# The second LSTM step of window pairs as seven half-size products in place of eight, with four groups' rows parked in DRAM

## The chip, the cores and the metric

The kernel runs on one core of one Trainium2 chip. The metric is the device time of one execution in microseconds; the median of three runs of the kernel before is 2540.0 us (2535.27 to 2540.68). The profile shown is of one execution with a span of 2539.1 us at a mean granted TensorE clock of 0.993, so the clock plays no part here.

## What is computed

The input is a batch of 128 graphs of 64 nodes with 256 features, 8192 rows in all, in fp32. Four layers follow one another, each with a residual sum and a layer norm: two kinds of graph convolution, a convolution with LSTMs over windows of nodes, and an attention. The change lies in the third layer, whose core is

```python
for p in range(1, 4 + 1):
    nw = Tv // p
    wins = h[:, :nw * p, :].reshape(Bv * nw, p, Hd)
    last = _lstm_last(Wih[p - 1], Whh[p - 1], bih[p - 1], bhh[p - 1], wins)
    h = h.at[:, arange(nw) * p + (p - 1), :].set(last)
# one step of _lstm_last
g = x_t @ Wih.T + h @ Whh.T + bias          # 1024 gate columns out of 256 + 256
i, f, gg, o = split(g, 4)
c = sigmoid(f) * c + sigmoid(i) * tanh(gg)
h = sigmoid(o) * tanh(c)
```

For p = 2 the 64 nodes of a graph make 32 windows of two nodes. The first step has no previous state, so it needs `Wih` alone. The second step needs `Wih` and `Whh`, and it is this step that changes.

## The kernel before

The rows are cut into 64 tiles of 128 and handled in 16 **groups** of four tiles, that is eight graphs or 512 rows. All rows lie in the SBUF tile `X` (L649) from start to end and are updated in place.

The program has two stages. In the first, `layer0` runs for all groups, two at a time, with a Strassen scheme of its own for its largest product. There a `norms` list holds small pieces of layer-norm work; one piece is popped for each of the 14 products of a group (L832). Beside it `eigen`, a long chain of small VectorE instructions, works out a 64 x 64 eigenbasis. In the second stage, from about 860 us on, `group(g)` takes each group through `layer1`, `layer2` and `layer3`; three groups are under way at once (`WAYS = 3`).

**What sets the order.** TensorE's order is written out by hand (L1205 to L1219): each group is a generator that yields the time at which its next piece may start, on a clock `now` that the program advances by its own price for each matmul (L717). The loop picks the first group that is ready, in the order in which the groups began, and if none is ready it moves the clock to the one that is ready soonest. The waiting times are constants, such as `CELL[256] = 3.8` us after the last matmul of an LSTM step with 256 moving columns. TensorE itself knows nothing of `now`: it runs its list in order and waits only where an operand or a buffer isn't ready. The orders of VectorE and ScalarE are left to the framework's scheduler in this stage.

**The LSTM** is `lstm(hT, p, first, nw)`, L991. `hT` holds the group's nodes transposed, with features on the partitions. For each step `t` it goes through eight `units` (L1005), one for each gate and half of the gate's 256 columns. A unit takes one PSUM bank from `ps4`, fills it with two matmuls of `wi` and, from the second step on, two of `wh` (L1026, L1029), each with all `n = 8 * nw` moving columns. Then one ScalarE tanh reads the bank with bias (L1030), and VectorE works out `c` and `h` from the gate tiles (L1034 to L1041, L1051). For p = 2 there are 256 moving columns. Every bank of the LSTM is first written in full and then read, and it has no second writer before it is given back. The pool `psb` has eight banks[...]; `pw` has five tiles with tag `w`.

## Time and profile before

| what | us | share of the span |
|---|---|---|
| TensorE matmul, busy | 2494.8 | 98% |
| TensorE weight load, busy | 2196.2 | 86% |
| VectorE, busy | 1407.8 | 55% |
| ScalarE, busy | 1090.6 | 43% |
| DMA, mean rate | 12 GB/s | |

In the stage that holds the change, between 900 and 2300 us, VectorE is busy for about 92 us in each 200 and ScalarE for about 90. The DMA queues are all but silent after the inputs and weights have been loaded, at the start and at 845 to 870 us.

A fp32 matmul call of the program appears as two MATMUL instructions in the profile: the second step of p = 2 has 8 units x 2 calls of `whh` for 16 groups, 256 calls, and the profile lists 512 such instructions. The duration of one matmul in the profile overlaps that of the next, so what one costs on the way is the distance from start to start. A group of instructions is listed as line, engine, operation, output and inputs with their shapes and a count; then the busy time, the mean duration of one in ns, and the idle time just before them with what ended it.

### The profile page before, as it was taken

Reading aid. Unit: us, or ns where it says so; the run is one execution under the profiler, and the core shown is the slowest. Engines: PE = TensorE matmul, PEld = TensorE weight load, DVE = VectorE, ACT = ScalarE, POOL = GpSimd, SP = SyncE. Lnnn points to the kernel's source line nnn. Section 1 sums busy time; section 2 is a strip of 40 time slices with the busy share of each in tenths; the row PEclk is TensorE's granted clock in tenths of the full one; section 3 lists DMA queues with packets and bytes.
Section 4 is the critical chain, followed back from the end, with each engine's and each line's share of the span. In section 5 each row is a group of like instructions: output and inputs, shape, how many; then the busy total and the mean of one; then the engine's idle time right before and its main releaser. Section 6 shows DMA issues by size and latency. Waiting matters only on the chain.

```text
span 2539.1 us, 39015 instructions
## 1 busy us (share of the span) xinstructions
PE 2494.8 (98%) x15020; PEld 2196.2 (86%) x15020; DVE 1407.8 (55%) x4996; ACT 1090.6 (43%) x2706; POOL 134.2 (5%) x316
## 2 busy tenths in 40 slices
PE   9999999999999999999999999999999999999997
PEld 7788887888878889998989889898998998978996
DVE  6888777778885433454453543544445345353235
ACT  2344333433333344445344444444444534535454
POOL 0000000000000100000000000000000000010001
PEclk9999999999999999999999999999999999999998
DMA  6000000000000300000000000000000000000000
GB/s 219 1 1 1 1 1 1 1 1 1 1 1 1 117 1 1 10 9 1 9 9 1 9 1 10 9 1 9 1 9 9 1 9 9 1 9 1 1 1 26
DMA packets 24634, 32.09 MB, mean 13 GB/s; under 512 B 2176, under 2 KB 21376, under 8 KB 24448
## 3 DMA queue, kind: packets, MB, share of 16 engines
q1 hardware_dynamic: 24096, 29.32, 3.4%
q8 instruction: 118, 1.93, 0.3%
q14 instruction: 68, 0.56, 0.1%
q10 hardware_dynamic: 352, 0.28, 0.0%
HBM read 21.20 MB, written 8.39 MB: 12 GB/s over the span
## 4 chain that ended last, share of the span: by engine, by line
PE 91%; DVE 5%; POOL 2%; issue 1%; DMA 0%; ACT 0%; SPq 0%; ACTq 0%; POOLq 0%; DVEq 0%
PE ps L716 88%; PE ps L926 2%; POOL ln_rs L554 1%; DVE X L564 1%; DVE ln_st L551 1%; DVE D L51 1%; PE ps L1146 1%; PE pc L93 1%; DMA X<-in_x_dram 0%; POOL ln_rs L553 0%; DVE tw L51 0%; DVE ln_mv L552 0%; DVE X L1176 0%; DVE X L986 0%; DVE X L1096 0%
## 5 line engine op out<-in xcount | busy, mean ns | idle before, releaser
L716 PE MATMUL ps<-w,wih 128*128 128x256 f32 (+2 forms) x4992 | 894.0, 319 | 1.8 <-DVE w L1051 1.8
L716 PEld LDWEIGHTS ps<-w,wih 128*128 128x128 f32 x4992 | 760.9, 191 | 47.8 <-issue 5.7
L1030 ACT ACTIVATE gates<-ps,cbi 128x128 f32<-128x128 f32 (+2 forms) x1248 | 499.3, 410 | 523.3 <-PE ps L716 516.2
L716 PE MATMUL ps<-hs,whh 128*128 128x128 f32 (+2 forms) x3072 | 540.5, 303 | 6.2 <-DVE hs L1041 6.2
L716 PEld LDWEIGHTS ps<-hs,whh 128*128 128x128 f32 x3072 | 453.9, 191 | 32.9 <-issue 11.2
L1036 DVE SCALAR_TENSOR_TENSOR gates<-gates 128x256 f32<-128x256 f32 (+2 forms) x256 | 89.3, 349 | 297.4 <-ACT gates L1030 297.4
L716 PE MATMUL ps<-aw,h 128*128 128x256 f32 x1024 | 227.2, 379 | 0.0
L716 PEld LDWEIGHTS ps<-aw,h 128*128 128x128 f32 x1024 | 192.9, 190 | 25.9 <-ACT h L725 0.5
L725 ACT ACTIVATE h<-h 128x512 f32<-128x512 f32 x128 | 80.5, 629 | 170.0 <-DVE h L51 169.8
L1039 ACT ACTIVATE gates<-c 128x128 f32<-128x128 f32 (+2 forms) x288 | 98.1, 341 | 114.1 <-DVE c L1038 87.9
L1034 DVE SCALAR_TENSOR_TENSOR c<-gates,c 128x128 f32<-128x128 f32 (+2 forms) x192 | 62.6, 326 | 139.4 <-ACT gates L1030 138.2
L1051 DVE SCALAR_TENSOR_TENSOR w<-gates 128x256 f32<-128x256 f32 (+2 forms) x160 | 59.6, 376 | 108.5 <-PE ps L716 73.5
L716 PE MATMUL ps<-ss,tw 128*128 128x256 f32 x512 | 117.9, 380 | 0.0
L716 PE MATMUL ps<-ss,aw 128*128 128x256 f32 x512 | 117.3, 379 | 0.0
L716 PE MATMUL ps<-m,aw 128*128 128x256 f32 x512 | 117.1, 380 | 0.0
L716 PE MATMUL ps<-aw,m 128*128 128x512 f32 x256 | 114.8, 594 | 0.0
L1041 DVE SCALAR_TENSOR_TENSOR hs<-gates 128x128 f32<-128x128 f32 (+2 forms) x192 | 62.6, 326 | 93.6 <-ACT gates L1039 52.4
L553 POOL TENSOR_SCALAR ln_rs<-ln_mv 128x2 f32<-128x2 f32 x96 | 26.2, 273 | 1558.4 <-DVE ln_mv L552 1557.9
L716 PEld LDWEIGHTS ps<-ss,aw 128*128 128x128 f32 x512 | 96.6, 190 | 12.8
L716 PEld LDWEIGHTS ps<-ss,tw 128*128 128x128 f32 x512 | 96.3, 190 | 12.9 <-issue 0.2
L564 DVE TENSOR_SCALAR X<-X,ln_mv,ln_rs 128x256 f32<-128x256 f32 x176 | 64.7, 410 | 75.9 <-POOL ln_rs L554 75.9
L716 PEld LDWEIGHTS ps<-m,aw 128*128 128x128 f32 x512 | 95.6, 190 | 12.6 <-issue 0.5
(294 smaller groups left out, 3107.4 us busy)
## 6 DMA issues: line engine op xcount, KB each, us to landing
X<-in_x_dram SPq DMA_DIRECT2D x30, 256.0 KB, 6.3
out_dram<-X SPq DMA_DIRECT2D x28, 256.0 KB, 2.1
wih<-in_c_ih_dram SPq DMA_DIRECT2D x4, 1024.0 KB, 7.2
aw<-in_a_w_dram SPq DMA_DIRECT2D x3, 1024.0 KB, 10.3
whh<-in_c_hh_dram SPq DMA_DIRECT2D x3, 1024.0 KB, 9.4
out_dram<-X SPq DMA_DIRECT2D x8, 128.0 KB, 1.7
aw<-in_a_w_dram SPq DMA_DIRECT2D x1, 512.0 KB, 5.8
cw<-in_c_w_dram SPq DMA_DIRECT2D x2, 256.0 KB, 5.1
```

Source lines behind the costliest of these rows:

```text
L51: return getattr(self.engine, name)(out, *args, **kw)
L553: nc.gpsimd.tensor_scalar(rs, mv[:, :, 1], EPS, None, op0=ALU.add)
L564: nc.vector.tensor_scalar(x[:, t, :], x[:, t, :], mv[:, t, 0:1], rs[:, t:t + 1], op0=ALU.subtract, op1=ALU.mult)
L716: PE.matmul(out, lhsT, rhs, start=start, stop=stop)
L725: S.activation(dst, src, AF.Relu)
L926: PE.transpose(out, in_, ident)
L1030: S.activation(gate[q][:, h, :], pp, AF.Tanh, bias=bias[:, j:j + 1], scale=0.5 if q == "g" else 0.25)
L1034: V.scalar_tensor_tensor(c[:, h, :], gate["f"][:, h, :], 1.0, c[:, h, :], op0=ALU.add, op1=ALU.mult)
L1036: V.scalar_tensor_tensor(to, gate["i"][:, h, :], 1.0, gate["g"][:, h, :], op0=ALU.add, op1=ALU.mult)
L1039: S.activation(gate["i"][:, h, :], c[:, h, :] if p > 1 else to, AF.Tanh, scale=0.5)
L1041: V.scalar_tensor_tensor(new[:, h, :], gate["o"][:, h, :], 1.0, gate["i"][:, h, :], op0=ALU.add, op1=ALU.mult)
L1051: V.scalar_tensor_tensor(hT[:, h, slice(first + p - 1, first + nw * p, p), :], gate["o"][:, h, :].rearrange("p (w b) -> p w b", b=8), 1.0, ...
```

## The change

The second step of p = 2 is one matrix product: 1024 gate columns, 512 contraction rows (256 of `x`, 256 of `h`) and 256 moving columns. It is computed by Strassen's scheme, in Winograd's form: gates, contraction and moving rows are each cut in halves (i and g against f and o; the first against the second 128 features, in `x` and in `h` alike; windows 0 to 15 against 16 to 31). Seven products of half-size operands take the place of eight. It is for taking matmul work off TensorE. For this it needs sums of weight quarters, made once (`sums`, `add_weights`), differences of moving operands, made for each group (`less`), and additions of the products on VectorE before the tanh can be taken from SBUF.

The weight sums take 16 KB of each partition. To make room for them, `X` keeps 12 groups' rows instead of 16. The first stage begins with groups 12 to 15; when one has gone through it, its rows are stored to a DRAM tile `rest`, and groups 0 to 3 are loaded into their place. In the second stage, when group 0 to 3 has ended, the rows of group 12 to 15 are loaded back.

```diff
+LATE = 4
-    X = keep.tile([P, NT, D], F32, name="X")
+    X = keep.tile([P, NT - 4 * LATE, D], F32, name="X")
+    rest = [aside.tile([P, 4, D], F32, name=f"rest{i}") for i in range(LATE)]
+    order = list(range(NT // 4 - LATE, NT // 4)) + list(range(NT // 4 - LATE))
...
+        def change():
+            nc.sync.dma_start(rest[g], xs)
+            for t in (0, 2):
+                nc.sync.dma_start(xs[:, t:t + 2, :], given(order[g + LATE])[:, t:t + 2, :])
...
+        if g < LATE:
+            norms.append(change)
...
+    sums = [wb.tile([P, 4, 2, 2, P], F32, name=f"sums{i}") for i in range(2)]
+    def add_weights():
+        for w, s in zip((wih[1], whh[1]), sums):
+            a11, a12, a21, a22 = quarters(w)
+            V.tensor_add(s[:, 0], a21, a22)
...
+    def second(hT, xt, hs, G, c, bias, ready):
...
+        both = tl(pw, [P, 1024], "w").rearrange("p (s i n) -> p s i n", s=2, i=4)
...
+                V.tensor_sub(T[2], b2[1], b1[1])
+                V.tensor_sub(T[1], b2[1], T[0])
+                V.tensor_sub(T[3], b2[0], T[1])
...
+        yield ready
+        for h in range(2):
+            p12, p43, p57 = (ps4((P, 2, 2, P)) for _ in range(3))
+            p6 = ps4((P, 2, P))
+            into = (p12[:, 0], p12[:, 1], p43[:, 1], p43[:, 0], p57[:, 0], p6, p57[:, 1])
+
+            def product(i):
+                for q in range(2):
+                    for s in range(2):
+                        mm(into[i][:, q, :], ways[s][weight[i]][:, q, h, :], moving[i][s], s == 0, s == 1)
+
+            u1 = work2()[:, :256].rearrange("p (q n) -> p q n", q=2)
+            product(0)
+            S.copy(u1, p12[:, 0])
+            product(1)
+            product(2)
+            yield now[0]
+            a, b, c12, _ = (G[:, h, w, m] for w in range(2) for m in range(2))
+            product(5)
+            V.tensor_add(a, u1, p6)
+            product(6)
+            V.tensor_add(b, a, p57[:, 1])
+            yield now[0]
+            product(4)
+            V.tensor_add(G[:, h, 1], G[:, h, 0], p57[:, 0].unsqueeze(1).to_broadcast([P, 2, 2, P]))
+            V.tensor_add(a, u1, p12[:, 1])
+            V.tensor_add(c12, c12, p43[:, 1])
+            product(3)
+            V.tensor_add(b, b, p43[:, 0])
+            gate = {}
+            for m, q, name in ((1, 0, "f"), (0, 0, "i"), (0, 1, "g"), (1, 1, "o")):
...
+                S.activation(gate[name], gate[name], AF.Tanh, bias=bias[:, j:j + 1],
+                             scale=0.5 if name == "g" else 0.25)
...
+            yield now[0]
+        for h in range(2):
+            for w in range(2):
...
+                V.scalar_tensor_tensor(hT[:, h, 32 * w + 1:32 * w + 32:2, :], o, 1.0, i, op0=ALU.add, op1=ALU.mult)
+        return now[0] + CELL[256] + 1.0
...
+            if p == 2 and t:
+                ready = yield from second(hT, xt, hs, G, c, bias, ready)
+                break
...
+            elif g == 0:
+                add_weights()
...
+        if g < LATE:
+            nc.sync.dma_start(xs, rest[g])
```

`h` in `second` counts the two 128-column halves of a gate. Each half takes four PSUM banks, of which `p12`, `p43` and `p57` hold two products each.

More of the change, by code (lines that the diff above doesn't have):

```diff
@@ L647, in load, with rows_of, given @@
         return t
-    X = keep.tile([P, NT, D], F32, name="X")
+    X = keep.tile([P, NT - 4 * LATE, D], F32, name="X")
+    aside = ctx.enter_context(tc.tile_pool(name="aside", bufs=1, space=bass.MemoryType.DRAM))
+    rest = [aside.tile([P, 4, D], F32, name=f"rest{i}") for i in range(LATE)]
+    order = list(range(NT // 4 - LATE, NT // 4)) + list(range(NT // 4 - LATE))
+    def rows_of(g):
+        at = g % (NT // 4 - LATE)
+        return X[:, 4 * at:4 * at + 4, :]
+    def given(g):
+        return x_t[:, 4 * g:4 * g + 4, :]
     adst = keep.tile([P, N], F32, name="adst")
@@ L653 @@
     nc.sync.dma_start(adst[N:, :], adj)
-    nc.scalar.dma_start(X[:, 2:4, :], x_t[:, 2:4, :])
+    nc.scalar.dma_start(rows_of(order[0])[:, 2:4, :], given(order[0])[:, 2:4, :])
     for t in range(2):
-        nc.sync.dma_start(X[:, t, :], x_t[:, t, :])
+        nc.sync.dma_start(rows_of(order[0])[:, t, :], given(order[0])[:, t, :])
     aw1 = load(wa, "aw1", a_w1, "(k p) f -> p k f", [P, 2, 512], p=P)
@@ L662 @@
     aw3 = load(wa, "aw3", a_w3, "(k p) f -> p k f", [P, 8, D], p=P)
-    for t in range(4, NT, 2):
-        nc.sync.dma_start(X[:, t:t + 2, :], x_t[:, t:t + 2, :])
+    for g in order[1:LATE] + order[2 * LATE:]:
+        for t in (0, 2):
+            nc.sync.dma_start(rows_of(g)[:, t:t + 2, :], given(g)[:, t:t + 2, :])
     nc.sync.dma_start(eig_c, consts)
@@ L744, in layer0 @@
     def layer0(g):
-        xs = X[:, 4 * g:4 * g + 4, :]
+        xs = rows_of(order[g])
+        def change():
+            nc.sync.dma_start(rest[g], xs)
+            for t in (0, 2):
+                nc.sync.dma_start(xs[:, t:t + 2, :], given(order[g + LATE])[:, t:t + 2, :])
         def mixed(dst, src, nf, more, then=None):
@@ L914, with quarters @@
         whh.append(load(wb, f"whh{i}", c_hh[i], "(k p) f -> p k f", [P, 2, 1024], p=P) if i else None)
+    def quarters(w):
+        w = w.rearrange("p k (a b h m) -> p k a b h m", a=2, b=2, h=2)
+        return [w[:, k, :, b] for b in range(2) for k in range(2)]
+    sums = [wb.tile([P, 4, 2, 2, P], F32, name=f"sums{i}") for i in range(2)]
+    ways = [[quarters(w)[i] for i in (0, 1, 3)] + [s[:, i] for i in range(4)]
+            for w, s in zip((wih[1], whh[1]), sums)]
+    def add_weights():
+        for w, s in zip((wih[1], whh[1]), sums):
+            a11, a12, a21, a22 = quarters(w)
+            V.tensor_add(s[:, 0], a21, a22)
+            V.tensor_sub(s[:, 1], s[:, 0], a11)
+            V.tensor_sub(s[:, 2], a11, a21)
+            V.tensor_sub(s[:, 3], a12, s[:, 1])
     att = []
@@ L989, in layer1, with halves, less @@
         return ready
+    def second(hT, xt, hs, G, c, bias, ready):
+        G = G.rearrange("p (h w m q n) -> p h w m q n", h=2, w=2, m=2, q=2)
+        both = tl(pw, [P, 1024], "w").rearrange("p (s i n) -> p s i n", s=2, i=4)
+        def halves(b):
+            return b[:, 0:16], b[:, 16:32]
+        def less(s, b1, b2, part):
+            T = [both[:, s, i].rearrange("p (w b) -> p w b", b=8) for i in range(4)]
+            if 0 in part:
+                V.tensor_sub(T[0], b1[1], b1[0])
+            if 1 in part:
+                V.tensor_sub(T[2], b2[1], b1[1])
+                V.tensor_sub(T[1], b2[1], T[0])
+                V.tensor_sub(T[3], b2[0], T[1])
+        x1, x2 = (halves(b) for b in xt)
+        h1, h2 = (halves(hs[:, k, :].rearrange("p (w b) -> p w b", b=8)) for k in range(2))
+        less(0, x1, x2, (0, 1))
+        less(1, h1, h2, (0, 1))
+        T1, T2, T3, T4 = ([both[:, s, i].rearrange("p (w b) -> p w b", b=8) for s in range(2)] for i in range(4))
+        moving = ((x1[0], h1[0]), (x2[0], h2[0]), (x2[1], h2[1]), T4, T1, T2, T3)
+        weight = (0, 1, 6, 2, 3, 4, 5)
+        yield ready
[27 more added lines that the diff above has]
+            for m, q, name in ((1, 0, "f"), (0, 0, "i"), (0, 1, "g"), (1, 1, "o")):
+                j = 2 * "ifgo".index(name) + h
+                gate[name] = G[:, h, :, m, q, :]
+                S.activation(gate[name], gate[name], AF.Tanh, bias=bias[:, j:j + 1],
+                             scale=0.5 if name == "g" else 0.25)
+            ch = c[:, h, :].rearrange("p (w n) -> p w n", w=2)
+            V.scalar_tensor_tensor(ch, gate["f"], 1.0, ch, op0=ALU.add, op1=ALU.mult)
+            V.scalar_tensor_tensor(gate["g"], gate["i"], 1.0, gate["g"], op0=ALU.add, op1=ALU.mult)
+            V.scalar_tensor_tensor(ch, ch, 0.5, gate["g"], op0=ALU.mult, op1=ALU.add)
+            S.activation(gate["i"], ch, AF.Tanh, scale=0.5)
+            yield now[0]
+        for h in range(2):
+            for w in range(2):
+                o, i = (G[:, h, w, m, 0 if m == 0 else 1, :].rearrange("p (w b) -> p w b", b=8) for m in (1, 0))
+                V.scalar_tensor_tensor(hT[:, h, 32 * w + 1:32 * w + 32:2, :], o, 1.0, i, op0=ALU.add, op1=ALU.mult)
+        return now[0] + CELL[256] + 1.0
@@ L1002, in lstm @@
             names = "figo" if t else "igo"
-            G = tl(pg, [P, 2048], "gates")[:, :2 * len(names) * n].rearrange("p (q h n) -> p q h n", h=2, n=n)
+            G = tl(pg, [P, 2048], "gates")
+            if p == 2 and t:
+                ready = yield from second(hT, xt, hs, G, c, bias, ready)
+                break
+            G = G[:, :2 * len(names) * n].rearrange("p (q h n) -> p q h n", h=2, n=n)
             gate = {q: G[:, i] for i, q in enumerate(names)}
@@ L1187, in group @@
     def group(g):
-        xs = X[:, 4 * g:4 * g + 4, :]
+        xs = rows_of(g)
         ready = [0.0, 0.0]
```

## Prediction

> **What bounds the kernel now.** I read the page from the top: first the busy shares, then the chain that ended last, then the costliest groups, and last the timeline of the two places that the change touches.

> ```profile
> PE 2494.8 (98%) x15020; PEld 2196.2 (86%) x15020; DVE 1407.8 (55%) x4996; ACT 1090.6 (43%) x2706; POOL 134.2 (5%) x316
> ...
> PE 91%; DVE 5%; POOL 2%; issue 1%; DMA 0%; ACT 0%; SPq 0%; ACTq 0%; POOLq 0%; DVEq 0%
> ```

> TensorE is the bound: it is idle for 44 of 2539 us, and 91% of the chain lies on it. A microsecond of matmul that goes away is a microsecond won, and a microsecond that TensorE waits is one lost: its order is fixed, so nothing slips into a wait. The waits on record are few:

> ```profile
> PE ps L716 <- DVE X L564: 6.9, 5, 2.8
> PE ps L716 <- DVE hs L1041: 6.2, 5, 1.3
> ...
> PE ps L716 <- DVE w L1051: 1.8, 2, 1.5
> ```

> Columns: total us, times, longest. Next, the price of a matmul, from TensorE's timeline (start, us, instruction, count). The last part of a second step of p = 2 with 256 columns, then a step of p = 4 with 128:

> ```profile
> 1533.64 1.03 PE L716 MATMUL ps<-w,wih 128*128 128x256 f32 x4
> 1534.50 1.03 PE L716 MATMUL ps<-hs,whh 128*128 128x256 f32 x4
> 1535.37 1.03 PE L716 MATMUL ps<-w,wih 128*128 128x256 f32 x4
> 1536.23 1.03 PE L716 MATMUL ps<-hs,whh 128*128 128x256 f32 x4
> ...
> 1576.27 0.61 PE L716 MATMUL ps<-w,wih 128*128 128x128 f32 x4
> 1576.71 0.61 PE L716 MATMUL ps<-hs,whh 128*128 128x128 f32 x4
> 1577.16 0.61 PE L716 MATMUL ps<-w,wih 128*128 128x128 f32 x4
> ```

> Start to start, four instructions take 0.864 us with 256 columns (0.216 each, 0.432 a call) and 0.447 with 128 (0.112 each, 0.223 a call). Half the columns cost a little over half.

> The prices of the other engines:

> ```profile
> L1030 ACT ACTIVATE gates<-ps,cbi 128x256 f32<-128x256 f32 x416 | 192.8, 472 | 219.4 <-PE ps L716 218.3
> L1039 ACT ACTIVATE gates<-c 128x256 f32<-128x256 f32 x64 | 26.6, 415 | 49.3 <-DVE c L1038 39.4 <-DVE c L1036 9.5
> L971 DVE TENSOR_TENSOR v<-ps,wide_b_b 128x256 f32<-128x256 f32 x32 | 13.2, 414 | 4.8 <-PE ps L716 4.8
> L986 DVE TENSOR_TENSOR X<-ps,X 128x512 f32<-128x512 f32 x32 | 21.1, 676 | 0.5 <-PE ps L716 0.5
> L1041 DVE SCALAR_TENSOR_TENSOR hs<-gates 128x128 f32<-128x128 f32 x96 | 27.9, 291 | 44.1 <-ACT gates L1039 37.0 <-ACT gates L1030 4.1 <-PE ps L716 2.8
> ```

> So a VectorE addition costs 0.29, 0.41 or 0.68 us at 128, 256 or 512 elements.

> [...] 1.03 us shown for four against 0.864 of distance; so I price by distance. [...] The kernel before never reads one part of an LSTM bank while another part is still to be written, so its trace can't say. The forecast rests on this.

> **Matmuls.** Removed, per group: 8 units x 4 calls x 0.432 = 13.82 us. Added: 7 products x 2 halves x 2 x 2 = 56 calls x 0.223 = 12.50. Gain 1.33 us a group, x16 = **21 us**. That is all there is to win.

> **Waits within `second`.** The new step puts two products into one bank and reads the first before the second is written. If a bank has one user at a time, TensorE, which has no yield in between, waits. From the timeline: ScalarE and VectorE start 0.20 us after the last matmul is through (matmuls end at 1535.37, tanh starts at 1535.57), and TensorE starts 0.05 after the release (copy L979 ends at 1196.36, matmul at 1196.41). Per half:
> - product(1) into `p12` waits for the copy of product(0): 0.20 + 0.45 + 0.05 = **0.70**. The copy of 256 elements isn't in the trace; it lies between 0.415 and 0.472 of the two tanh rows.
> - product(4) into `p57` waits for the addition that reads product(6): 0.20 + 0.41 + 0.05 = **0.66**. A yield stands before it, so an older group's matmuls may fill it. How often, the trace can't say; I take half (bounds none and all).
> - product(3) into `p43` waits for `c12`, which stands third on VectorE after product(4): 0.20 + 0.68 + 0.41 + 0.41 + 0.05 = **1.75**. No yield.

> Per half 0.70 + 0.33 + 1.75 = 2.78, x32 = 89 us. VectorE and ScalarE are busy half the time with other groups' work in pieces of 0.3 to 0.7 us; I add 0.2 per wait, x96 = 19 us (bounds 0 and 40). In the second half the copy finds ScalarE at the first half's tanhs (4 x 0.415 us, starting 0.6 us into product(0)); bounds 0 and 1.5, I take 0.5 x16 = 8 us. Behind each wait in TensorE's queue stand all three groups' matmuls. **Sum: 116 us.**

> **After `second`.** From the last matmul to the last write of `hT`: VectorE 0.61, tanhs f, i, g 1.25, two VectorE operations 0.84, tanh 0.42, two writes 0.58, hand-overs some 0.5: 4.2 to 5.2 us, where before it took 1.45 (matmuls through at 1537.09, L1051 done at 1538.54). The planner allows 4.8 instead of 3.8; before, p = 3 came 4.35 and 3.5 us after in the two cases I followed. Bounds 0 and 1.5 us a group; 0.5 x16 = **8 us**. Against that the start of `second` is eased: product(0) needs only the first half of `hs`, and the first difference is needed 12 calls, 2.7 us, later; `less` on `hs` is 4 x 0.29 = 1.2 us. And where TensorE waits anyway, other groups' chains catch up: of the 44 us idle now I take **8 us** off.

> **Work hidden beside TensorE.** VectorE gains per group 8 x 0.29 for `less`, 2 x (5 x 0.41 + 0.68) for the additions and 0.3 for the split writes, 8.1 us; from 46% to 54% in this stage. ScalarE gains two copies, and loses 8 x 0.057 since the tanh reads SBUF. Neither becomes the bound. `add_weights`, 8 x 0.68 = 5.5 us of VectorE once, stands behind group 0's p = 1 matmuls while three groups run: 0 to 5 us, I take 0. The tile `both` is a sixth possible claimant of five `w` tiles only if two others hold two each at that moment: 0.

> **DRAM.** A parked group is 512 KB out and 512 KB in: by the rows of the DMA list (256 KB store 2.1 us, load 6.3 us) below 20 us on an idle queue. The slot is needed again four groups of some 54 us (860/16) later; in the second stage some 1300 us lie between. `change` lengthens the `norms` list by four pieces, with no work for TensorE. I cost all this at nothing.

> **Sum.** 2540 - 21 + 116 + 8 - 8 = 2635. I predict **2633 us**, 3.7% slower.

> **The rivals.**
> - A, no waits at shared banks (the products use different columns). Then 2540 - 21 + 8 + 2 for the switch of stages = 2529: **faster**. For it speaks the plain data flow, in which no product depends on another's reader[...]. Chance 0.10.
> - B, waits exist but half is filled: yields are used by older groups each time, the engines are free and p = 2 falls where TensorE had waits before. 2540 - 21 + 78 (0.70 + 1.75 alone, x32) - 8 = 2589. In the trace second steps do run interleaved now and then. Chance 0.15.
> - C, the copy stands in ScalarE's queue behind the whole first half, its last tanh included, and VectorE's other work falls between: 1.9 us more per group for the copy, 0.4 more per half for VectorE, 2633 + 30 + 13 + 12 for the chain = 2688. Chance 0.12.
> - D, waits and gain cancel, 2540: 0.03. It would take waits of 0.65 us a half, less than any one of the three; only a stray case.

> The forecast has the remaining 0.60. The range reaches from B to C, 2585 to 2692; A, D and the outer edges stay out, some 0.17. Faster 0.10 (A), same 0.03 (D), slower 0.87.

> **What would show it.** In the waits of TensorE new rows must stand: on the ScalarE copy into `v` some 32 times with 0.7 us or more, and on VectorE's additions into `gates` some 50 to 64 times, up to 2 us each, together over 80 us. The second step must span some 19 us rather than 13.8 where uninterrupted. The 0.112 us from start to start must hold within a product. TensorE's busy time must fall, its idle time grow. Wrong, if those rows are missing and TensorE's idle stays near 44 us: then A holds. If the waits name DMA or X, the parking is the cause instead.

## The result, and the profile after

The kernel after takes **2719.8 us** (median; 2717.3 to 2724.0) where the kernel before takes 2537.9 in the same runs: a ratio of 1.0718, interval 1.0698 to 1.0738. Slower, as forecast, and by twice as much: 182 us where 93 were predicted, and outside the range.

The page of the kernel after, busy times and shares of the chain that ended last:

```profile
PE 2534.8 (93%) x15788; PEld 2244.6 (83%) x15788; DVE 1531.5 (56%) x5356; ACT 1106.2 (41%) x2738; POOL 139.9 (5%) x316
...
PE 85%; DVE 9%; POOL 2%; ACT 1%; issue 1%; DMA 0%; SPq 0%; ACTq 0%; POOLq 0%; DVEq 0%
```

VectorE has 9% of the chain where it had 5. The profiled span is 2718.1 us, so TensorE is idle for 183.3 us instead of 44.3: **139 us more idle time**. But its busy time has risen too, from 2494.8 to 2534.8, by 40 us, although 21 us of matmul were taken out. **So some 61 us are lost while TensorE works**, and no wait shows them.

First the idle part. The waits of TensorE (total us, times, longest):

```profile
PE ps L731 <- DVE gates L1087: 94.2, 32, 5.9
PE ps L731 <- ACT v L1074: 16.8, 32, 0.9
PE ps L731 <- DVE w L1172: 15.1, 10, 1.5
PE ps L731 <- DVE gates L1082: 14.2, 17, 3.8
PE ps L731 <- ACT v L1023: 8.4, 12, 1.0
```

L1074 is the copy of product(0), L1082 the second addition into `b`, L1087 the addition into `c12`: the three readers behind which the prediction put product(1), product(4) and product(3). Together they are 125.2 us. L1172 is the write of `hT` that ends p = 1, for which p = 2 waits, and L1023 a copy in `layer1`: 1.8 and 0.7 us before (there L1051 and L979), 23.5 now.

The wait on L1087 has a floor of 1.57 us, but nine of the second halves wait 5.87. One of them on VectorE's timeline (start, us, line; in brackets the idle time before and who ended it):

```profile
1379.38 0.73 DVE L566 TENSOR_SCALAR X<-X,ln_mv,ln_rs 128x256 f32<-128x256 f32 x2 [0.76 <-POOL ln_rs L556]
1380.04 0.75 DVE L553 BATCH_NORM_STATS2 ln_st<-X 128x6 f32<-128x256 f32 x2
1380.70 0.17 DVE L554 BATCH_NORM_AGGREGATE ln_mv<-ln_st 128x2 f32<-128x6 f32 x1
1380.78 0.66 DVE L1085 TENSOR_TENSOR gates<-gates,ps 128x512 f32<-128x512 f32 x1
1381.35 0.18 DVE L554 BATCH_NORM_AGGREGATE ln_mv<-ln_st 128x2 f32<-128x6 f32 x1
1381.47 0.42 DVE L1086 TENSOR_TENSOR gates<-v,ps 128x256 f32<-128x256 f32 x1
1382.65 0.73 DVE L566 TENSOR_SCALAR X<-X,ln_mv,ln_rs 128x256 f32<-128x256 f32 x2 [0.76 <-POOL ln_rs L556]
1383.31 0.41 DVE L1087 TENSOR_TENSOR gates<-gates,ps 128x256 f32<-128x256 f32 x1
```

The three additions that TensorE needs, L1085 to L1087, last 1.5 us together. Between and ahead of them stands another group's layer norm, which itself waits twice for GpSimd (0.76 us each). VectorE is not short of time: from 1381.89 to 1382.65 it stands idle for 0.76 us although L1087 has its operands, and L1087 starts only at 1383.31, behind L566. In this timeline what VectorE could do next stands behind what can't start.

The same moment on TensorE:

```profile
1383.77 0.80 PE L731 MATMUL ps<-w,wih 128*128 128x128 f32 x2 [5.87 <-DVE gates L1087]
1384.36 0.63 PE L731 MATMUL ps<-w,whh 128*128 128x128 f32 x2
1384.79 0.64 PE L731 MATMUL ps<-w,wih 128*128 128x128 f32 x2
1385.21 0.63 PE L731 MATMUL ps<-w,whh 128*128 128x128 f32 x2
```

and a first half, 16 us earlier, with the next three starts:

```profile
1368.07 0.49 PE L731 MATMUL ps<-w,wih 128*128 128x128 f32 x2 [2.03 <-DVE gates L1087]
1368.40 0.39 PE L731 MATMUL ps<-w,whh 128*128 128x128 f32 x2
1368.62 0.39 PE L731 MATMUL ps<-w,wih 128*128 128x128 f32 x2
1368.85 0.39 PE L731 MATMUL ps<-w,whh 128*128 128x128 f32 x2
```

Start to start, the same call takes 0.43 us after the long wait and 0.223 after the short one: **half speed**. The trace's clock records say so as well: TensorE had half its clock for 39.8 us of the kernel before (4 stretches), and for 152.4 us of the kernel after (24 stretches, of 3.4, 6.8 or 10.2 us but for the last); about 2 us of each total lie behind the last instruction. Only the part of a stretch in which TensorE worked is counted as a loss. The sums of busy time over these stretches, before and then after:

```profile
sum 37.74, PE 23.48 PEld 19.79 DVE 15.64 ACT 10.90 POOL 7.05; mean PE 5.87 PEld 4.95 DVE 3.91 ACT 2.72 POOL 1.76
sum 150.31, PE 103.39 PEld 96.20 DVE 69.46 ACT 45.32 POOL 13.39; mean PE 4.31 PEld 4.01 DVE 2.89 ACT 1.89 POOL 0.56
```

Half of the 80 us more (103.4 against 23.5) is **40 us lost by the clock**, an estimate from the two prices of a call, 0.43 and 0.223 us. The other 21 of the 61 lie at the edges of the stops. In this line of the kernel before, a running matmul of 128 columns lasts 0.275 us, while the next starts 0.112 us after it:

```profile
L716 PE MATMUL ps<-w,wih 128*128 128x128 f32 x1920 | 269.3, 275 | 0.0
```

At a stop no next one comes, so 0.16 us of the stop count as busy. After the stop, at full clock, the second instruction starts 0.213 us after the first and not 0.112. Together this is 0.26 us at each of 32 + 17 + 32 = 81 stops, an estimate of 21 us.

### The profile page after: what moved, and what is told of

Its sections match the earlier page's. It is cut to its first block, busy times and chain, and to the rows that moved or that the text cites. A ratio compares the mean times of both kernels' runs of the same rounds, so it can differ in the third digit from the quotient of the medians.

```text
span 2718.1 us, 40991 instructions
## 1 busy us (share of the span) xinstructions
PE 2534.8 (93%) x15788; PEld 2244.6 (83%) x15788; DVE 1531.5 (56%) x5356; ACT 1106.2 (41%) x2738; POOL 139.9 (5%) x316
## 3 DMA queue, kind: packets, MB, share of 16 engines
q8 instruction: 124, 2.03, 0.3%
## 4 chain that ended last, share of the span: by engine, by line
PE 85%; DVE 9%; POOL 2%; ACT 1%; issue 1%; DMA 0%; SPq 0%; ACTq 0%; POOLq 0%; DVEq 0%
PE ps L731 82%; POOL ln_rs L556 2%; DVE X L566 1%; PE ps L970 1%; DVE ln_st L553 1%; DVE gates L1085 1%; DVE D L51 1%; DVE X L1219 1%; POOL ln_rs L555 1%; PE ps L1269 1%; DVE ln_mv L554 1%; PE pc L93 1%; DMA X<-in_x_dram 0%; ACT gates L1094 0%; DVE X L1299 0%
## 5 line engine op out<-in xcount | busy, mean ns | idle before, releaser
L731 PE MATMUL ps<-w,wih 128*128 128x128 f32 (+2 forms) x4864 | 864.2, 315 | 126.8 <-DVE gates L1087 94.2
L731 PEld LDWEIGHTS ps<-w,wih 128*128 128x128 f32 x4864 | 738.9, 195 | 177.2 <-DVE gates L1087 100.4
L1151 ACT ACTIVATE gates<-ps,cbi 128x128 f32<-128x128 f32 (+2 forms) x1120 | 442.2, 404 | 464.1 <-PE ps L731 457.8
L731 PE MATMUL ps<-hs,whh 128*128 128x128 f32 (+1 forms) x2816 | 465.5, 289 | 5.8 <-DVE hs L1162 5.8
L731 PEld LDWEIGHTS ps<-hs,whh 128*128 128x128 f32 x2816 | 403.3, 194 | 9.1 <-DVE hs L1162 6.1
L1157 DVE SCALAR_TENSOR_TENSOR gates<-gates 128x128 f32<-128x128 f32 (+2 forms) x224 | 76.0, 339 | 248.5 <-ACT gates L1151 248.4
L1094 ACT ACTIVATE gates<-gates,cbi 128x256 f32<-128x256 f32 x128 | 58.3, 502 | 206.3 <-DVE gates L1087 165.4
L731 PE MATMUL ps<-w,sums 128*128 128x128 f32 x896 | 124.7, 280 | 14.2 <-DVE gates L1082 14.2
L731 PEld LDWEIGHTS ps<-w,sums 128*128 128x128 f32 x896 | 112.3, 193 | 19.2 <-DVE gates L1082 17.5
L1155 DVE SCALAR_TENSOR_TENSOR c<-gates,c 128x128 f32<-128x128 f32 (+1 forms) x160 | 49.3, 308 | 109.6 <-ACT gates L1151 109.0
L566 DVE TENSOR_SCALAR X<-X,ln_mv,ln_rs 128x256 f32<-128x256 f32 x176 | 64.7, 410 | 77.8 <-POOL ln_rs L556 77.7
```

Source lines behind the costliest of these rows:

```text
L566: nc.vector.tensor_scalar(x[:, t, :], x[:, t, :], mv[:, t, 0:1], rs[:, t:t + 1], op0=ALU.subtract, op1=ALU.mult)
L731: PE.matmul(out, lhsT, rhs, start=start, stop=stop)
L1094: S.activation(gate[name], gate[name], AF.Tanh, bias=bias[:, j:j + 1], scale=0.5 if name == "g" else 0.25)
L1151: S.activation(gate[q][:, h, :], pp, AF.Tanh, bias=bias[:, j:j + 1], scale=0.5 if q == "g" else 0.25)
L1155: V.scalar_tensor_tensor(c[:, h, :], gate["f"][:, h, :], 1.0, c[:, h, :], op0=ALU.add, op1=ALU.mult)
L1157: V.scalar_tensor_tensor(to, gate["i"][:, h, :], 1.0, gate["g"][:, h, :], op0=ALU.add, op1=ALU.mult)
```

## The experiments

**Theory**: each of the three waits follows from a bank that has one user at a time; VectorE's queue lengthens one of them; and the waits cost a second time through the clock. **Rivals**: the parked rows and the weight sums are the cause; or the loss is the load on the other engines and the long chain after the last product, which would stay if the waits at the banks went.

The diffs are against the kernel after, in `second` unless told otherwise. Each ratio is to the kernel before on the same chip.

**Parking and weight sums kept, second step as before** (`park`):

```diff
-            if p == 2 and t:
+            if False:
```

> The rows are parked in DRAM, and the weight sums are made, as in the changed kernel; the second step of p = 2 is the old one, with eight units. Theory of the shared banks: parking and sums cost nothing, so the time is that of the kernel before, 2538 us within 0.3%, with TensorE idle near 44 us and the clock near 0.993. Theory of the parking (the moved rows, the longer list of norm pieces or the DRAM traffic slow the stages): most of the 180 us stays, above 2600 us.

Measured: 2539.5 us, ratio 1.001 (1.0003 to 1.0017). Parking, sums and the longer list of norms cost some 2.5 us (0.8 to 4.3). All the rest of the loss lies in the Strassen step.

**The reads moved behind the second product of their bank** (`reads_late`; `c12_late` moves only the last of the three):

```diff
-            S.copy(u1, p12[:, 0])
             product(1)
+            S.copy(u1, p12[:, 0])
...
-            V.tensor_add(b, a, p57[:, 1])
...
             product(4)
...
+            V.tensor_add(b, a, p57[:, 1])
...
-            V.tensor_add(c12, c12, p43[:, 1])
             product(3)
+            V.tensor_add(c12, c12, p43[:, 1])
```

> The changed kernel, but each read of a bank with two products stands behind the second product: the copy of product(0) behind product(1), the addition of product(6) behind product(4), the addition of c12 behind product(3). Same matmuls, same VectorE and ScalarE work. Theory of the shared banks: the 125 us of waits on these three reads go, and with them the half-speed stretches of the TensorE clock; 2525 to 2545 us, idle below 60 us. Theory of the load (eight microseconds more of VectorE work a group and a longer chain behind the step are what costs): above 2650 us.

> The changed kernel with one line moved: the addition of c12 stands behind product(3). Theory of the shared banks, with the waits as the trace has them: the 94 us on this read go, and some 40 us of half-speed clock that follow them, so 2570 to 2610 us; the waits on the copy (17 us) and on the addition of product(6) (14 us) stay. If the wait were only passed on to the next operand, above 2680 us.

Measured: `reads_late` 2605.3, ratio 1.0268 (1.0251 to 1.0285); `c12_late` 2651.3, ratio 1.0451 (1.0436 to 1.0467). Both missed. The wait of TensorE that is longest in `reads_late`:

```profile
PE ps L731 <- DVE w L1105: 44.9, 10, 5.0
```

and in `c12_late`:

```profile
PE ps L731 <- DVE w L1105: 42.8, 9, 4.8
PE ps L731 <- ACT v L1074: 18.6, 32, 1.8
```

The moved reads no longer stop TensorE, which shows that the waits came from reading a bank between its two products: in `reads_late` L1074, L1082 and L1087 are all gone, and the kernel is 114 us shorter than the kernel after. In every run the two products of a bank are also one tile of the program (`p12`, `p43`, `p57`), so whether the dependency goes by the bank or by the tile isn't told apart.

But a new wait of nearly 5 us has come up nine times, on L1105, the write of `hT` that ends the step and that p = 3 needs. The additions still stand behind a layer norm of another group in VectorE's queue, and behind a copy (L997), as here:

```profile
1342.06 0.66 DVE L1085 TENSOR_TENSOR gates<-gates,ps 128x512 f32<-128x512 f32 x1
1343.27 0.73 DVE L566 TENSOR_SCALAR X<-X,ln_mv,ln_rs 128x256 f32<-128x256 f32 x2 [0.56 <-POOL ln_rs L556]
1343.92 0.68 DVE L997 COPY w<-ps 128x512 f32<-128x512 f32 x1
1344.53 0.41 DVE L1086 TENSOR_TENSOR gates<-v,ps 128x256 f32<-128x256 f32 x1
```

Before, TensorE waited for it inside the step; now it runs ahead and meets the delay at the end. In `c12_late` 43 of the 94 us were handed on in this way. So the rival had half a point: a slow chain was hidden behind the waits.

**Work put into the wait** (`fill`): four matmuls of 256 columns into `p6`, which has been read by then, ahead of product(3). Nothing reads their result.

```diff
+        moving_any = wih[0][:, 0, 0:256].rearrange("p (q n) -> p q n", q=2)
...
+            for _ in range(4):
+                PE.matmul(p6, ident, moving_any, start=True, stop=True)
             product(3)
```

> The changed kernel with four more matmuls of 256 columns, identity by weights, into the bank of product(5) (read by then, its content is not used again) between product(4) and product(3): 1.73 us of extra TensorE work in each of the 32 waits of 2.94 us, so nothing becomes shorter by data flow. Theory of the clock (idle stretches halve TensorE's clock for some microseconds and that cost some 56 of the 180 us): fewer half-speed stretches, 2670 to 2700 us. If the clock does not matter: 2720 us or more.

Measured: 2703.5, ratio 1.0659 (1.0643 to 1.0675), 3.5 us above the band expected. 128 matmuls of 0.432 us are 55 us of work that nobody needs, and the kernel is 16 us **faster** than without. What is left of that wait:

```profile
PE ps L731 <- DVE gates L1088: 40.7, 20, 4.1
```

Idle time fell by 51 us, to 132.6; busy time rose by only 35 where 55 were added, so 20 us came back from the clock. The half-speed time fell from 152 to 89 us (granted clock 0.972 and 0.984), and TensorE's busy time within it from 103 to 62, half of which is 21. (The 56 us in the expectation counted idle time at half clock too.)

**Only the order on VectorE** (`prio`; `prio_fill` adds three matmuls as above):

```diff
-            V.tensor_add(c12, c12, p43[:, 1])
+            with tc.high_priority(offset=1500): V.tensor_add(c12, c12, p43[:, 1])
```

and likewise for the two additions above it, L1085 and L1086; nothing else.

> The changed kernel with only VectorE's order altered: the additions of product(4), a and c12 are put ahead of another group's layer norm in its queue. Theory of the queue: of the 94 us on the read of c12, about 39 us (9 waits of 5.9 us instead of 1.6) come from that norm, which waits for GpSimd in front of them; these waits fall to about 2 us each, and some of the half-speed clock goes with them, so 2650 to 2690 us. If the 5.9 us were the bank's own price: 2720 us as before.

> As the run with VectorE's order altered (2678 us), with three more matmuls of 256 columns into the bank of product(5), whose content is not used again, between product(4) and product(3): 1.30 us of TensorE work in each of the 32 waits of 1.57 to 2.0 us, so data flow gains nothing from it. Theory of the clock: waits of under 0.8 us are left at that place, half-speed stretches fall from 104 us towards 60, and the time falls by 10 to 22 us, to 2656 to 2668 us, though TensorE does 41 us more work. If the clock does not follow the waits: 2678 us or more.

Measured: `prio` 2678.2, ratio 1.0558 (1.0542 to 1.0574); `prio_fill` 2658.1, ratio 1.047 (1.0452 to 1.0487). Both as expected. In `prio`:

```profile
PE ps L731 <- DVE gates L1087: 59.3, 32, 2.0
```

That is 1.85 us each, 2.0 counted from start to start, where the prediction had 1.75 and 0.2 for the queue: without the norm in front the wait has the size that was worked out, and 35 us of the 94 were the queue alone.

`prio` is also the clearest view of the clock. From TensorE's timeline, around one wait:

```profile
1699.69 0.80 PE L731 MATMUL ps<-w,wih 128*128 128x128 f32 x2 [2.03 <-DVE gates L1087]
1700.28 0.63 PE L731 MATMUL ps<-w,whh 128*128 128x128 f32 x2
1700.70 0.63 PE L731 MATMUL ps<-w,wih 128*128 128x128 f32 x2
...
1702.41 0.60 PE L731 MATMUL ps<-w,wih 128*128 128x128 f32 x2
...
1704.02 0.39 PE L731 MATMUL ps<-hs,whh 128*128 128x128 f32 x2
1704.24 0.39 PE L731 MATMUL ps<-w,wih 128*128 128x128 f32 x2
```

and the same stretch by windows (length, busy us of PE, PEld, DVE, ACT and POOL, then the granted clock, the DMA share and GB/s):

```profile
1696.50:1699.70 3.20, 1.17 (x9) 0.98 (x9) 2.28 (x6) 0.86 (x3) 0.00 (x0) 0.96 0.00 0
1699.70:1703.10 3.40, 3.40 (x16) 3.34 (x16) 1.17 (x4) 1.72 (x4) 0.00 (x0) 0.54 0.00 0
1703.10:1706.50 3.40, 2.94 (x27) 2.81 (x26) 1.04 (x4) 1.13 (x4) 0.00 (x0) 1.00 0.02 5
```

After this wait of 2.03 us the clock is halved for 3.4 us, 16 instructions instead of some 30. Of the 19 waits of 2.03 or 2.04 us on L1087 in this trace, 16 have a half-speed stretch that begins within 1.5 us of their end; of the 13 of 1.56 to 1.80 us, one has (at 1019.64), and another, at 1252.92, ends within a stretch that was already under way. One of the 16 ends at 1712.62, with no other wait of TensorE in the 8 us ahead of it.

In `prio_fill`, whose TensorE does 96 x 0.432 = 41 us more, that wait and the busy time are:

```profile
PE ps L731 <- DVE gates L1088: 17.6, 31, 0.7
```

```profile
PE 2541.7 (96%) x15980; PEld 2241.4 (84%) x15980; DVE 1523.4 (57%) x5356; ACT 1102.9 (42%) x2738; POOL 140.9 (5%) x316
```

`prio` has 2527.1 us busy. So 41 us of work raised the busy time by 15; the half-speed time fell from 104 us to 38 (granted clock 0.981 and 0.993), and no stretch follows any of the 31 shortened waits. The kernel got 20 us faster by doing more. Work put into the waits shortens nothing else, so some 20 us are what the long waits had cost here through the clock, besides their own length.

**Other mates in the banks** (`paired`): the products are so paired and ordered that both of a bank are written before either is read, with other products meanwhile where the chain allows it. The two yields move with them.

```diff
-            p12, p43, p57 = (ps4((P, 2, 2, P)) for _ in range(3))
-            p6 = ps4((P, 2, P))
-            into = (p12[:, 0], p12[:, 1], p43[:, 1], p43[:, 0], p57[:, 0], p6, p57[:, 1])
+            p12, p43, p67 = (ps4((P, 2, 2, P)) for _ in range(3))
+            p5 = ps4((P, 2, P))
+            into = (p12[:, 0], p12[:, 1], p43[:, 1], p43[:, 0], p5, p67[:, 0], p67[:, 1])
...
             product(0)
+            product(1)
             S.copy(u1, p12[:, 0])
-            product(1)
-            product(2)
-            yield now[0]
             a, b, c12, _ = (G[:, h, w, m] for w in range(2) for m in range(2))
             product(5)
-            V.tensor_add(a, u1, p6)
+            yield now[0]
             product(6)
-            V.tensor_add(b, a, p57[:, 1])
+            V.tensor_add(a, u1, p67[:, 0])
+            V.tensor_add(b, a, p67[:, 1])
+            product(4)
+            V.tensor_add(G[:, h, 1], G[:, h, 0], p5.unsqueeze(1).to_broadcast([P, 2, 2, P]))
+            V.tensor_add(a, u1, p12[:, 1])
             yield now[0]
-            product(4)
-            V.tensor_add(G[:, h, 1], G[:, h, 0], p57[:, 0].unsqueeze(1).to_broadcast([P, 2, 2, P]))
-            V.tensor_add(a, u1, p12[:, 1])
-            V.tensor_add(c12, c12, p43[:, 1])
+            product(2)
             product(3)
-            V.tensor_add(b, b, p43[:, 0])
+            bc = G[:, h].rearrange("p w m q n -> p (w m) q n")[:, 1:3]
+            V.tensor_add(bc, bc, p43)
```

> The changed kernel with other bank mates and another order of products: 1 and 2, then 6 and 7, then 5 alone, then 3 and 4, so that no bank is read between its two products; products 3 and 4 are added by one VectorE operation of 512 elements. Theory of the shared banks: no waits on the reads within the step. What is left is the chain after the step, one operation shorter than with the reads moved (2605 us): 2560 to 2600 us. Theory of the load: no gain over 2605 us.

Measured: 2571.7, ratio 1.0143 (1.0126 to 1.016), as expected. No product waits at a bank any more. The longest wait of TensorE in `paired` is the following, before 15.0 us on L1172:

```profile
PE ps L731 <- DVE w L1105: 23.1, 9, 2.6
```

**The same, with priority for every VectorE and ScalarE operation of the step behind the differences of `less`** (`paired_prio`; `tc.high_priority(offset=1500)` for each, as in `prio`), **and with p = 3 planned later as well** (`paired_prio2`; `paired_prio3` later still, `paired2` without the priority):

```diff
-        return now[0] + CELL[256] + 1.0
+        return now[0] + CELL[256] + 2.5
```

This is the time from which the planner takes the next step of the group: 6.3 us after the last product instead of 4.8; `paired_prio3` has `+ 4.0`, 7.8 us.

> As the run with other bank mates, and in addition all VectorE and ScalarE operations of the step stand ahead of other groups' work in their queues. Theory of the queue: the waits of p = 3 on the last writes of the step (45 us with the reads moved) go as well, since they come from another group's norm in front: 2525 to 2560 us, with the clock back near 0.99. If the chain itself is too long for the 4.8 us that the planner allows, over 2570 us.

> As the run before, with 6.3 us instead of 4.8 us allowed by the planner after the step. If the other groups have work for that time, the last waits go: 2518 to 2540 us, up to 21 us of matmul time below the kernel before. If all three groups are waiting then, the time stays as without it.

> Other bank mates without the altered queue order (2572 us), but 6.3 us instead of 4.8 us allowed after the step. Theory of the queue: the last writes are late by another group's norm in front of them, whatever the planner allows; the wait of 2.6 us nine times shrinks by what the planner fills, to 2540 to 2565 us. If the allowance alone was short: as good as with both, 2515 to 2525 us.

> Other bank mates, altered queue order, and 7.8 us allowed after the step (2518 us with 6.3). The waits there are gone already, so no more to gain from this: 2510 to 2526 us; over 2530 us if the longer allowance leaves the planner without ready groups.

Measured:

| kernel | us | ratio to before (interval) | p = 3 planned after |
|---|---|---|---|
| `paired` | 2571.7 | 1.0143 (1.0126 to 1.016) | 4.8 us |
| `paired_prio` | 2537.9 | 1.0005 (0.9997 to 1.0014) | 4.8 us |
| `paired2` | 2531.8 | 0.9972 (0.9961 to 0.9983) | 6.3 us |
| `paired_prio2` | **2518.4** | **0.9927 (0.9912 to 0.9942)** | 6.3 us |
| `paired_prio3` | 2550.9 | 1.0045 (1.003 to 1.006) | 7.8 us |

`paired_prio` and `paired_prio2` came as expected, `paired2` and `paired_prio3` did not. `paired_prio2` beats both kernels. Its page:

```profile
PE 2475.3 (98%) x15788; PEld 2203.2 (88%) x15788; DVE 1516.1 (60%) x5324; ACT 1090.4 (43%) x2738; POOL 142.4 (6%) x316
```

TensorE's busy time is 19.5 us below that of before, and its idle time, 2516.8 - 2475.3 = 41.5 us, is no longer: the gain that was worked out for the matmuls is all there once nothing eats it. The waits of the others say what was left. In `paired_prio` the wait on L1105 is gone and the longest is

```profile
PE ps L731 <- DVE w L1172: 15.0, 10, 1.5
```

and in `paired2`, where L1172 is gone instead:

```profile
PE ps L731 <- DVE w L1105: 7.6, 9, 0.9
```

From `paired` to `paired_prio2` 53 us are won. Priority alone gives 34 and the later plan 19.5 more; the later plan alone gives 40 and priority 13 more. They overlap, since both serve the same chain; `paired2` was expected to show which of the two it is, and fell between. `paired_prio3` missed on the wrong side:

```profile
PE ps L731 <- DVE w L997: 14.7, 13, 1.8
PE ps L970 <- DVE X L566: 7.6, 5, 1.7
```

With p = 3 held back for 7.8 us, TensorE meets waits in other groups instead. That fits a planner that runs out of ready work, as that expectation said; it was argued from the places of the waits, and not tried further.

## Why the prediction was right in direction and wrong in size

- **The matmuls**: 21 us predicted. The busy time of `paired_prio2` shows 19.5. Right.
- **One user of a bank at a time**: the forecast's direction rests on it. It was an assumption, which the trace of before could not show. In the kernel after TensorE waits at each of the three reads, 32, 17 and 32 times, and in `paired` at none. Here are the sizes of these waits. The prediction priced a matmul from start to start, so its waits must be counted in the same way: by how much the start after the stop comes later than 0.112 us. The shortest are 0.62 us for the copy, 0.67 for one addition and 1.73 for three, where 0.70, 0.66 and 1.75 were worked out. These prices were right; the copy takes 370 ns, not 450. As idle time the profile lists 0.46, 0.51 and 1.57 of them:

```profile
L1074 ACT COPY v<-ps 128x256 f32<-128x256 f32 x32 | 11.8, 370 | 19.2 <-PE ps L731 19.1
```

- **The sum of these waits**: 116 us predicted. Counted from start to start it is some 146: 125 us idle and 21 at the edges of the stops. Product(1) took 25 where 22 and 8 for ScalarE's tail stood; the tail is hardly there, as 26 of the 32 waits are the shortest. Product(4) took 19 where 11 stood, with 17 of 32 left unfilled against half assumed, three of them 1.2 to 3.8 us long. Product(3) took 103 where 56 stood. **The term that was mis-sized is the 0.2 us of queue for each wait**, 19 us in all: at product(3) alone the queue costs 94.2 - 32 x 1.57 = 44 us, above the bound of 40. The prediction took VectorE's other work as pieces of 0.3 to 0.7 us that come at random. It did not ask whether such a piece can itself wait, as the norm does for GpSimd. An overestimate at product(1) took some of it back. The slow second instruction after each stop, 8 us in all, is a term that the prediction did not have.
- **After the step**: 8 us for p = 3 and 8 us won back elsewhere, so nothing. No wait on L1105 showed in the kernel after, since TensorE was late itself: where the reads were moved, it came up. The rest of the idle time grew by 139 - 125 = 14 us: L1172 and L1023 by 21, a place the prediction did not name, while the other waits fell by 7, close to the 8 taken off. L1172 keeps its 15 us with other bank mates and with priority, and loses them when p = 3 is planned later (`paired2`), so they hang on the planned order and not on the banks.
- **The clock: the step that is missing.** The prediction priced a wait at its length, and every matmul at full speed ("The 0.112 us from start to start must hold within a product"; TensorE's busy time "must fall"). After the long waits it did not hold: 0.43 us instead of 0.223 a call. Some 40 us, and busy time rose by 40 instead of falling by 21. The trace of before gave little sign of this, at a granted clock of 0.993; that the clock plays no part was true of that kernel alone.
- **Work beside TensorE and the parking**: costed at nothing. `park` measures some 2.5 us for parking and sums; in `paired_prio2`, with the additions on VectorE, TensorE's idle time is no longer than before. Right. One reading was wrong without harm to the sum: the tanh of the gates out of SBUF was to be 0.057 us shorter than out of PSUM, and is longer, 502 ns against 474:

```profile
L1094 ACT ACTIVATE gates<-gates,cbi 128x256 f32<-128x256 f32 x128 | 58.3, 502 | 206.3 <-DVE gates L1087 165.4 <-DVE gates L1089 40.9
```

With the clock (40), the waits (30) and the rest of the idle time (14), 84 us are added to the 95 of the prediction's sum (2635; 2633 was named): 179, as between the two profiles. The queue's part was tried by `prio`, the clock's by `fill` and `prio_fill`; the edges of the stops are an estimate.

## What to carry to other kernels

Where two products share a PSUM bank, choose the mates by when they are read: write both, then read both, with other matmuls in between (2571.7 us in `paired` against 2719.8). When TensorE must wait for another engine, look at what stands ahead of the awaited instruction in that engine's order, above all at an instruction that itself waits for a third engine (5.87 us instead of 1.57 at L1087); then put the awaited ones first, and plan the next step for the length of the whole chain, not much beyond it. Price a stop of TensorE twice, from start to start and by the half clock that may follow it (0.43 us instead of 0.223 a call, in 16 of the 19 cases of 2.03 us in `prio`), and read the clock before asking why busy time has grown.

## What the runs showed of the hardware

In `prio` a half-speed stretch begins within 1.5 us of the end of 16 of the 19 waits of 2.03 or 2.04 us on L1087: around the one that ends at 1699.69 it lasts 3.4 us, and the one that ends at 1712.62 has no other wait in the 8 us ahead of it. One begins so at one of the 13 waits of 1.56 to 1.80 us, and in `prio_fill` at none of the 31 of up to 0.74 us.

| idle time in the window | windows | next window at half speed |
|---|---|---|
| up to 1.68 us | 1415 | 0 |
| 1.73 to 1.85 us | 9 | 4 |
| 1.98 us and more | 20 | 20 |

After a window at half speed the clock was back in all 24 cases with up to 0.55 us idle, and in none of 19 with 0.66 us or more. The wait of 2.03 us at 1368.07 in the kernel after, which no stretch follows, is cut by an edge of these windows, with 0.24 us in one and 1.79 in the next. So, by an estimate, are the three in `prio` that no stretch follows (1363.29, 1488.98 and 1588.00): counted back in steps of 3.413 us from the stretch that begins at about 1699.4, an edge falls in each, and at most some 1.8 us of it lie on one side. What decides between 1.73 and 1.85 us these traces leave open.
